# Four-column steps of the norms, the tangent and the ball on GpSimd in the first 14 of 16 groups, with a new order of the work

## The chip, the cores and the metric

The kernel runs on one core of a Trainium2 chip. The metric is the device time of one execution in microseconds; for the kernel before it is the median of three runs.

## The reference

128 graphs of 64 nodes, 256 features each, go through four layers. Each ends with the same residual and norm.

```python
x = _layernorm(x + gated_graph(x, adj, ...))    # 5 rounds: m = h @ W_l; agg = A^T m; h = GRU(agg, h)
x = _layernorm(x + graph_mlp(x, adj, ...))      # (eps * x + adj @ x) @ W1, RMS norm, silu, @ W2
x = _layernorm(x + project(expmap0(adj @ logmap0(x))))
x = _layernorm(x + attention(x, adj, ...))      # exp(e_i + f_j) on the edges, normalised, times h
```

The third layer is hyperbolic. `logmap0(x)` is the row `x` times `arctanh(min(n, 1 - 1e-7)) / n`, with `n` the row's length; the kernel calls it the tangent. `expmap0(u)` is `u` times `tanh(n)/n`, and `project` shortens rows that are longer than 0.996; together they are the ball. The layer norm subtracts the mean and divides by `sqrt(var + 1e-5)`. All of these need, for each row of 256 features, a few numbers only: mean, variance, length, factor.

## The kernel before, in words

**Tiles.** Two graphs make a block of 128 rows, which lie on the 128 partitions. Four blocks (`NB`) make a group, so there are 16 groups. A group's tile of rows is 128 x 4 x 256. A number for each row is a tile of 128 partitions x 4 columns (`tiny`), and a step on such a tile is called a four-column step here.

**What a group does**, in `group(g)`: five gated rounds (`gated`, matmuls at L800 and L806, in a Strassen-like form, with the sums of blocks `tA` and `tB` of `sums` made on VectorE, L345; between rounds VectorE transposes (L762) and 4 transfers (L675) bring the state back to rows as `hr`); the first norm; the aggregation and the two-layer network (`p_ah`, `p_bh`, `p_ch` at L983, squares at L969 whose sums GpSimd adds, L348, TensorE's `ps_ss` and a power on GpSimd at L1025, then scaling, silu and `ps_o`); the second norm; the tangent (L1051 to L1076), which scales the rows (L1080, L1081) for `ps_sup`; the ball (L1096 to L1112), which gives the factor `th` for the rows of L696; the third norm; the attention (`ps_a`, `ps_att`); the fourth norm and the output.

**The norm**, `layer_norm`: for groups 0 to 13 (`summed`) the row sums come with the sum that makes the rows. VectorE makes the mean with its sign turned (L712), ScalarE squares the rows around it and adds (L714), VectorE makes variance plus epsilon (L717), GpSimd raises it to −1/2 (L725, and to +1/2 for the second norm, which wants the row's length too), VectorE makes the length (L727) and the offset (L729). Groups 14 and 15 use VectorE's statistics instead of the sums (L721 to L723).

**The tangent and the ball.** VectorE limits the length, forms (1+n)/(1−n) with two reciprocals (L1053 to L1059); ScalarE takes Ln (L1061); VectorE sums a series for short rows (L1067 to L1072) and picks one of the two (L1074, L1076). In the ball GpSimd takes the root of the sum of squares (L1097), VectorE limits it (L1098), ScalarE takes tanh (L1099), and VectorE does a reciprocal (L1111) and six steps (L1105 to L1110).

**What sets the order.** Every operation is entered in a `Flow` with its engine, an estimated cost, and what it reads and writes. `Plan` then simulates the engines: it goes through time, and of the operations that are ready on each engine, from up to four groups at once (`WINDOW`), takes the one with the earliest start, and of several the first by a rank. `CHOICES` is a string of digits, one for each `STRETCH` microseconds of planned time, that says which rank counts there: group first, latest group first, or, for each entry of `LAGS`, the group's number times that lag less the longest path still ahead in the group. `HOPS` is what the plan adds between an operation and one on another engine that needs it. An operation marked `port` shares a port in the plan: GpSimd's and some of VectorE's don't overlap. The order found is then fixed for every engine's queue with dependencies (`BEHIND`); each engine works through its queue in that order, and an instruction that waits holds those behind it.

```python
    def pool(us, run, w, r=()):
        flow.op("POOL", us, run, w, r, port=True)
```

Of the kernel before, what the change touches and what calls it, by code (L numbers as in the profile page):

```python
# [128 lines left out]
class Flow:  # L129
# [11 lines left out]
    AHEAD = {"PE": 32, "DVE": 10, "ACT": 10, "POOL": 4, "SP": 2}  # L141


    HOPS = {"from PE": 0.22, "to PE": 0.15, "else": 0.06, "own": 0.0}

    SOONER = 0.4

# [2 lines left out]
    TRANSFERS = 8  # L150

    TABLE = 1.28
    WINDOW, STRETCH, LAGS = 4, 4.0, (60.0,)
    CHOICES = ("0001000220200211121122221102222222012010000101100010000000111101000111011110021011111000000111010210"
               "1211020210001002202110011000111212202011211020002100022200100101202020200112021110010111111000120211"
               "1102220002201010201110112001200101100101212111101011111001000010011100121121112020120101000000002220"
               "0010111020001121221202112100001010010120000001221112100000011000001001100000201221212001000010111110"
               "1101001100121020222110100210001101100000111100011011020110001000002010012201001001200010012002111101"
               "000201000111111111111102122110011000000100100110000111111011000011000")

    BEHIND = mybir.DependencyInfo(mybir.DependencyClass.NoSync, mybir.DependencyReason.DATA)

# [41 lines left out]
            u.then.append(o)  # L204
        self.ops.append(o)

    def hop(self, e, to):
        if e == to:
            return 0.0 if e == "PE" else self.HOPS["own"]
        return self.HOPS["from PE" if e == "PE" else "to PE" if to == "PE" else "else"]  # L210

    def ways(self):

        for i, o in enumerate(o for s in self.streams for o in s):
            o.id = i
        path = {}
        for ops in self.streams:
            longest = 0.0
            for o in reversed(ops):
                path[o] = o.us + max((path[u] + self.hop(o.eng, u.eng) for u in o.then if u.stream == o.stream), default=0.0)  # L220
                o.way = longest = max(longest, path[o])

    def issue(self):
# [17 lines left out]
def kernel(  # L241
# [31 lines left out]
    nc = tc.nc  # L273
    B, N, D = x.shape
# [3 lines left out]
    NB = 4  # L278
# [44 lines left out]
    def dve(n, run, w, r, port=False):  # L323
        flow.op("DVE", 0.145 + 0.00105 * n, run, w, r, port=port)
# [3 lines left out]
    def act(n, run, w, r, sets=None):  # L328
        flow.op("ACT", 0.22 + 0.00077 * n, run, w, r, sets=sets)
# [11 lines left out]
    def pool(us, run, w, r=()):  # L341
        flow.op("POOL", us, run, w, r, port=True)

    def summing(n, o, x0, x1, op, w, r):
        dve(n, lambda: nc.vector.tensor_tensor(o(), x0(), x1(), op), w, r, True)  # L345

# [21 lines left out]
    def over(t, n):  # L368
        return t.unsqueeze(1).to_broadcast([P, n, t.shape[-1]])
# [39 lines left out]
    eps2 = const.tile([P, 2, NB], F32, name="eps2")  # L409
# [214 lines left out]
    def group(g):  # L624
# [76 lines left out]
        def layer_norm(y, st, tag, name, norm=None):  # L701

            mv = tiny("mv", (P, NB, 2))
            ve, rstd, off = tiny("ve", (P, 2, NB)), tiny("rstd", (P, 2, NB)), tiny("off")
            o = rows(tag, f"x_{name}")
            m = 2 if norm else 1

            def row(b):
                return [(y, b)]

            if summed:
                dve(4, lambda: nc.vector.tensor_scalar(mv[:, :, 0], st[:, :, 0], -1.0 / D, None, OP.mult), [mv], [st])  # L712
                for b in range(NB):
                    act(400, lambda b=b: nc.scalar.activation(  # L714
                        o[:, b, :], y[:, b, :], AF.Square, bias=mv[:, b, 0:1], accum_out=st[:, b, 1:2]),
                        [(o, b), (st, (1, b))], [*row(b), mv])
                dve(8, lambda: nc.vector.scalar_tensor_tensor(  # L717
                    ve[:, :m, :], over(st[:, :, 1], m), 1.0 / D, eps2[:, :m, :NB], OP.mult, OP.add), [ve], [st])
            else:
                for b in range(NB):  # L720
                    dve(256, lambda b=b: nc.vector.bn_stats(st[:, b, :], y[:, b, :]), [(st, b)], row(b))  # L721
                    dve(4, lambda b=b: nc.vector.bn_aggr(mv[:, b, :], st[:, b, :]), [(mv, b)], [(st, b)])
                dve(8, lambda: nc.vector.tensor_tensor(  # L723
                    ve[:, :m, :], over(mv[:, :, 1], m), eps2[:, :m, :NB], OP.add), [ve], [mv])
            pool(1.25, lambda: nc.gpsimd.tensor_tensor(rstd[:, :m, :], ve[:, :m, :], pow2[:, :m, :NB], OP.pow), [rstd], [ve])  # L725
            if norm:
                dve(4, lambda: nc.vector.scalar_tensor_tensor(  # L727
                    norm.tile(), rstd[:, 1, :], float(np.sqrt(D)), rstd[:, 0, :], OP.mult, OP.mult), [norm], [rstd])
            dve(4, lambda: nc.vector.scalar_tensor_tensor(  # L729
                off.tile(), mv[:, :, 0], 1.0 if summed else -1.0, rstd[:, 0, :], OP.mult, OP.mult), [off], [mv, rstd])  # L730
# [306 lines left out]
        for h in range(2):  # L1037
# [11 lines left out]


        rn, fac, n2, ser = (tiny(t) for t in ("rn", "fac", "n2", "ser"))  # L1051
        near = tiny("near", dt=I32)
        dve(4, lambda: nc.vector.scalar_tensor_tensor(xn.tile(), xn.tile(), MIN_NORM, xn.tile(), OP.max, OP.max), [xn], [xn])  # L1053
        dve(4, lambda: nc.vector.reciprocal(rn.tile(), xn.tile()), [rn], [xn])
        dve(4, lambda: nc.vector.scalar_tensor_tensor(xn.tile(), xn.tile(), MAX_ARG, xn.tile(), OP.min, OP.min), [xn], [xn])

        dve(4, lambda: nc.vector.scalar_tensor_tensor(fac.tile(), xn.tile(), -1.0, one4[:, :NB], OP.mult, OP.add), [fac], [xn])
        dve(4, lambda: nc.vector.reciprocal(fac.tile(), fac.tile()), [fac], [fac])
        dve(4, lambda: nc.vector.scalar_tensor_tensor(fac.tile(), xn.tile(), 1.0, fac.tile(), OP.add, OP.mult),  # L1059
            [fac], [xn, fac])  # L1060
        act(4, lambda: nc.scalar.activation(fac.tile(), fac.tile(), AF.Ln), [fac], [fac], LN)  # L1061


        def series():
            v = nc.vector
            return [
                v.tensor_mul(n2.tile(), xn.tile(), xn.tile()),  # L1067
                v.scalar_tensor_tensor(ser.tile(), n2.tile(), 1.0 / 13.0, one4[:, :NB], OP.mult, OP.mult),
                *(v.scalar_tensor_tensor(ser.tile(), ser.tile(), 1.0 / q, n2.tile(), OP.add, OP.mult)
                  for q in (11, 9, 7, 5, 3)),  # L1070
                v.tensor_add(ser.tile(), ser.tile(), one4[:, :NB]),
                v.scalar_tensor_tensor(near.tile(), xn.tile(), SERIES_BELOW, one4[:, :NB], OP.is_lt, OP.mult)]  # L1072
        dve(1400, series, [n2, ser, near], [xn])
        dve(4, lambda: nc.vector.scalar_tensor_tensor(fac.tile(), fac.tile(), 0.5, rn.tile(), OP.mult, OP.mult),  # L1074
            [fac], [fac, rn])
        dve(4, lambda: nc.vector.copy_predicated(fac.tile(), near.tile(), ser.tile()), [fac], [fac, near, ser])  # L1076
        tan = rows("B", "tan")
        for b in range(NB):
            flow.either([
# [18 lines left out]
        dve(4, lambda: nc.vector.scalar_tensor_tensor(unb.tile(), un.tile(), MIN_NORM, un.tile(), OP.max, OP.max), [unb], [un])  # L1098
        act(64, lambda: nc.scalar.activation(th.tile(), unb.tile(), AF.Tanh), [th], [unb], TANH)  # L1099


        def onto_ball():
# [5 lines left out]
                v.reciprocal(un.tile(), un.tile()),  # L1108
                v.scalar_tensor_tensor(un.tile(), un.tile(), MAX_NORM, one4[:, :NB], OP.mult, OP.min),
                v.tensor_mul(th.tile(), th.tile(), un.tile())]  # L1110
        dve(4, lambda: nc.vector.reciprocal(urn.tile(), unb.tile()), [urn], [unb])  # L1111
        dve(900, onto_ball, [th, un], [th, un, urn])  # L1112
# [88 lines left out]
```

## Time and profile before

| What | Value |
|---|---|
| Median of 3 runs | 2306.16 us (2305.33 to 2307.16) |
| The profiled execution, its own time | 2305.08 us |
| Its span, first to last instruction | 2303.3 us |
| Granted clock of TensorE, mean | 0.993 |
| Busy: TensorE, VectorE, ScalarE, GpSimd | 2249.8, 1765.9, 1308.0, 339.1 us |

All views are of one profiled execution. PE is TensorE's matmul, PEld its weight load, DVE VectorE, ACT ScalarE, POOL GpSimd, SP SyncE. L696 is line 696 of the kernel; where a helper enters the operation, the line is the helper's, and the tile's name tells which step it is. In a row of groups the name after the operation is what is written, then what is read, then the shapes and the count; behind the bars stand the busy time, the mean of one in ns, and the idle time of the engine just before, with what ended it. In a timeline row the first two numbers are the start and the time in us. "x3" joins neighbouring instructions of one kind, and brackets hold the engine's idle time before and what ended it.

### The profile page before, as it was taken

To read this page: it belongs to the slowest core of one execution; us is meant where nothing else is said; L and a number is where in the kernel's file an instruction comes from. 1 tells how busy PE (TensorE), PEld (TensorE's weight loads), DVE (VectorE), ACT (ScalarE), POOL (GpSimd) and SP (SyncE) were. 2 spreads that over 40 slices of the span, in tenths; PEclk is the share of its full clock that TensorE was granted. 3 is DMA by queue.
4 is the path that set the end of the run, shared out by engine and by line. 5 is a ranking of instruction groups with operands and counts; after the bars stand their busy time and mean duration, and the time that the engine had idled before them with its cause. 6 is when DMAs were issued, how large, how long until landed. Compare 5 with 4: busy or idle time off the path is not lost.

```text
span 2303.3 us, 32320 instructions
## 1 busy us (share of the span) xinstructions
PE 2249.8 (98%) x11242; PEld 1973.5 (86%) x11242; DVE 1765.9 (77%) x4167; ACT 1308.0 (57%) x2797; POOL 339.1 (15%) x272
## 2 busy tenths in 40 slices
PE   9999999999999999999999999999999999999995
PEld 7888888888888888888788888888888888888874
DVE  6777788778688777777677778777877787867876
ACT  3444556665655555556565556646555566555564
POOL 2100202310110200202021021201110230110011
PEclk9999999999999999999999999999999999999997
DMA  5221112122213022102212212212122112212200
GB/s 145 28 33 28 28 23 54 19 49 28 49 28 58 10 31 55 28 19 40 46 40 28 49 28 30 47 19 48 29 28 45 32 19 49 54 14 28 46 10 19
DMA packets 428770, 84.20 MB, mean 37 GB/s; under 512 B 399124, under 2 KB 427824, under 8 KB 428608
## 3 DMA queue, kind: packets, MB, share of 16 engines
q1 hardware_dynamic: 426880, 80.26, 19.8%
q8 instruction: 89, 1.46, 0.3%
q10 hardware_dynamic: 1328, 1.31, 0.2%
q0 software_dynamic: 400, 0.57, 0.1%
q14 instruction: 73, 0.60, 0.1%
HBM read 32.55 MB, written 8.39 MB: 18 GB/s over the span
## 4 chain that ended last, share of the span: by engine, by line
PE 89%; DVE 6%; DMA 2%; SPq 1%; issue 1%; ACT 1%; POOL 0%; POOLq 0%; ACTq 0%; DVEq 0%
PE p_ga L800 22%; PE p_gc L800 11%; PE ps_o L315 9%; PE ps_agg L315 7%; PE p_hx L806 6%; PE p_gb L800 5%; PE p_ix L806 5%; PE p_ah L983 4%; PE p_iy L806 4%; PE p_hy L806 4%; PE ps_a L315 2%; PE p_ch L983 2%; DMA hr<-t 1%; SPq L675 1%; PE ps_wmih L315 1%; PE ps_sup L315 1%
## 5 line engine op out<-in xcount | busy, mean ns | idle before, releaser
L725 POOL TENSOR_TENSOR rstd<-ve,pow 128x4 f32<-128x4 f32 (+1 forms) x64 | 78.3, 1224 | 1097.5 <-DVE ve L717 1012.3
L315 PE MATMUL ps_o<-w2s,hid 128*128 128x256 f32 x1024 | 232.3, 379 | 0.4 <-ACT hid L1034 0.3
L315 PEld LDWEIGHTS ps_o<-w2s,hid 128*128 128x128 f32 x1024 | 193.8, 190 | 27.7 <-ACT hid L1034 1.5
L338 ACT ACTIVATE hnb<-p_hx,half_b 128x256 f32<-128x256 f32 x215 | 101.4, 471 | 146.1 <-PE p_hx L806 102.5
L800 PE MATMUL p_gc<-tA,w_h 128*128 128x256 f32 x640 | 172.4, 381 | 2.4 <-DVE y L696 2.4
L800 PE MATMUL p_ga<-tA,w_h 128*128 128x256 f32 x640 | 173.1, 379 | 0.0
L800 PE MATMUL p_gc<-tB,w_a 128*128 128x256 f32 x640 | 172.6, 380 | 0.2 <-DVE tB L345 0.2
L800 PE MATMUL p_ga<-tB,w_a 128*128 128x256 f32 x640 | 168.0, 379 | 0.7 <-DVE tB L345 0.7
L800 PE MATMUL p_ga<-agg,w_a 128*128 128x256 f32 x640 | 166.5, 379 | 0.0
L800 PE MATMUL p_ga<-hT,w_h 128*128 128x256 f32 x640 | 166.4, 379 | 0.0
L315 PEld LDWEIGHTS ps_agg<-edge,hr 128*128 128x128 f32 x1024 | 142.6, 192 | 24.5 <-issue 7.1
L315 PE MATMUL ps_agg<-edge,hr 128*128 128x128 f32 x1024 | 148.1, 278 | 7.0 <-DMA hr<-t 4.6
L853 ACT ACTIVATE U<-U,half_b 128x512 f32<-128x512 f32 (+1 forms) x160 | 94.3, 628 | 76.4 <-DVE U L850 76.3
L800 PEld LDWEIGHTS p_gc<-tA,w_h 128*128 128x128 f32 x640 | 120.9, 191 | 18.7 <-DVE y L696 2.8
L800 PEld LDWEIGHTS p_ga<-tB,w_a 128*128 128x128 f32 x640 | 120.6, 190 | 17.4 <-DVE tB L345 1.3
L800 PEld LDWEIGHTS p_gc<-tB,w_a 128*128 128x128 f32 x640 | 120.3, 190 | 16.5 <-DVE tB L345 0.8
L800 PEld LDWEIGHTS p_ga<-agg,w_a 128*128 128x128 f32 x640 | 119.9, 190 | 16.9 <-issue 1.0
L800 PEld LDWEIGHTS p_ga<-hT,w_h 128*128 128x128 f32 x640 | 119.2, 190 | 15.7 <-issue 0.5
L333 ACT COPY agg<-ps_agg 128x512 f32<-128x512 f32 x141 | 81.6, 579 | 87.8 <-PE ps_agg L315 85.4
L800 PEld LDWEIGHTS p_ga<-tA,w_h 128*128 128x128 f32 x640 | 117.2, 190 | 13.6
L853 ACT ACTIVATE V<-V,half_b 128x256 f32<-128x256 f32 (+1 forms) x160 | 86.6, 585 | 58.5 <-DVE V L850 58.1
L866 DVE TENSOR_TENSOR V<-p_ix,V 128x256 f32<-128x256 f32 x192 | 80.5, 419 | 33.5 <-PE p_ix L806 30.3
(261 smaller groups left out, 5466.0 us busy)
## 6 DMA issues: line engine op xcount, KB each, us to landing
hr<-t SPq DMA_DIRECT2D x256, 128.0 KB, 3.7
x<-in_x_dram SPq DMA_DIRECT2D x64, 128.0 KB, 2.6
xr<-in_x_dram SPq DMA_DIRECT2D x16, 512.0 KB, 4.3
out_dram<-x_n SPq DMA_DIRECT2D x16, 512.0 KB, 3.0
xs<-in_x_dram SPq DMA_DIRECT2D x120, 64.0 KB, 2.5
x3T<-t SPq DMA_DIRECT2D x56, 128.0 KB, 3.8
edge<-in_adj_dram SPq DMA_DIRECT2D x64, 32.0 KB, 2.2
wm<-in_L_gnn_weight_dram SPq DMA_DIRECT2D x5, 256.0 KB, 3.4
```

The lines of the kernel that those rows point to most:

```text
L315: return nc.tensor.matmul(o, lhsT, rhs, start=(k == 0), stop=(k == nk - 1))
L333: flow.either([("ACT", 0.22 + 0.00077 * n, lambda: nc.scalar.copy(o(), i())), ("DVE", 0.145 + 0.00105 * n, lambda: nc.vector.tensor_copy(o ...
L338: flow.either([("ACT", 0.3 + 0.0008 * n, lambda: nc.scalar.activation(o(), i(), AF.Identity, bias=bias(), scale=scale())), ("DVE", 0.145 + ...
L675: flow.op("SP", 0.6, lambda q=q: nc.sync.dma_start(view(dst.tile())[:, q], t[W * q:W * (q + 1)].rearrange("r m x d -> r m (x d)")), [(dst, ...
L725: pool(1.25, lambda: nc.gpsimd.tensor_tensor(rstd[:, :m, :], ve[:, :m, :], pow2[:, :m, :NB], OP.pow), [rstd], [ve])
L800: pe(HR, lambda i=i, w=w, c=c: nc.tensor.matmul(ps[:, c * HR:(c + 1) * HR], w[:, m, c * P:(c + 1) * P], v[i][0](), start=first and i == 1 ...
L806: pe(HR, lambda: nc.tensor.matmul(ps[:, j * HR:(j + 1) * HR], w[:, m, :], v[0](), start=first, stop=True, skip_group_check=True), [ps], [( ...
L853: act(HR if len(w) == 1 else R, lambda: nc.scalar.activation(o(), src(), AF.Tanh, bias=half_b[:, i * KD + c:i * KD + c + 1], scale=0.5), w ...
L866: dve(HR + 44, lambda: nc.vector.tensor_add(uu[:, c, half(n)], region(ps, j), uu[:, c, half(n)]), [(uu, (n, c))], [ps, (uu, (n, c))])
L983: pe(HR, lambda c=c: nc.tensor.matmul(ps[:, c * HR:(c + 1) * HR], w1f[:, w, (2 * q + c) * P:(2 * q + c + 1) * P], v[0](), start=first and ...
```

## The change

In the groups 0 to 13 nearly all four-column steps of the norms, the tangent and the ball go from VectorE to GpSimd. Two helpers, `few` and `few_s`, enter them with a planned cost of 0.25 us. Reciprocals become powers of −1, of which two share one instruction in the tangent. VectorE's fused steps fall apart into plain ones: a step of the series is a product and a sum, and the choice between Ln and series becomes `fac + near * (ser - fac)`. Groups 14 and 15 keep the old code. The planner's addition for a result on its way to TensorE goes from 0.15 to 0.42 us (the old value, as `REACH`, still serves for the longest paths), `STRETCH` goes from 4 to 7 us, `LAGS` has a second entry, and `CHOICES` is a new string of 328 digits in place of 569, so the order of all engines' queues is new.

```diff
-    HOPS = {"from PE": 0.22, "to PE": 0.15, "else": 0.06, "own": 0.0}
+    HOPS = {"from PE": 0.22, "to PE": 0.42, "else": 0.06, "own": 0.0}
+
+    REACH = {"from PE": 0.22, "to PE": 0.15, "else": 0.06, "own": 0.0}
...
-    WINDOW, STRETCH, LAGS = 4, 4.0, (60.0,)
...
+    WINDOW, STRETCH, LAGS = 4, 7.0, (60.0, 150.0)
...
-                path[o] = o.us + max((path[u] + self.hop(o.eng, u.eng) for u in o.then if u.stream == o.stream), default=0.0)
+                path[o] = o.us + max((path[u] + self.hop(o.eng, u.eng, self.REACH) for u in o.then if u.stream == o.stream), default=0.0)
...
+    def few(w, x0, x1, op, r):
+
+        pool(0.25, lambda: nc.gpsimd.tensor_tensor(w[0](), x0(), x1(), op), [w[1]], r)
+
+    def few_s(w, x, s0, op0, r, s1=None, op1=None):
+
+        pool(0.25, lambda: nc.gpsimd.tensor_scalar(w[0](), x(), s0, s1, op0, *((op1,) if op1 else ())), [w[1]], r)
...
+    less2 = const.tile([P, 2, NB], F32, name="less2")
+    nc.vector.memset(less2, -1.0)
...
-                dve(4, lambda: nc.vector.tensor_scalar(mv[:, :, 0], st[:, :, 0], -1.0 / D, None, OP.mult), [mv], [st])
+                few_s((lambda: mv[:, :, 0], mv), lambda: st[:, :, 0], -1.0 / D, OP.mult, [st])
...
-                dve(8, lambda: nc.vector.scalar_tensor_tensor(
-                    ve[:, :m, :], over(st[:, :, 1], m), 1.0 / D, eps2[:, :m, :NB], OP.mult, OP.add), [ve], [st])
+                few_s((lambda: ve[:, 0, :], (ve, 0)), lambda: st[:, :, 1], 1.0 / D, OP.mult, [st], LN_EPS, OP.add)
+                if norm:
+                    few_s((lambda: ve[:, 1, :], (ve, 1)), lambda: st[:, :, 1], 1.0, OP.mult, [st])
...
+            if summed:
+                few((lambda: off.tile(), off), lambda: mv[:, :, 0], lambda: rstd[:, 0, :], OP.mult, [mv, rstd])
+                if norm:
+                    few((lambda: norm.tile(), norm), lambda: rstd[:, 1, :], lambda: rstd[:, 0, :], OP.mult, [rstd])
+            else:
+                if norm:
+                    dve(4, lambda: nc.vector.scalar_tensor_tensor(
+                        norm.tile(), rstd[:, 1, :], float(np.sqrt(D)), rstd[:, 0, :], OP.mult, OP.mult), [norm], [rstd])
                 dve(4, lambda: nc.vector.scalar_tensor_tensor(
-                    norm.tile(), rstd[:, 1, :], float(np.sqrt(D)), rstd[:, 0, :], OP.mult, OP.mult), [norm], [rstd])
-            dve(4, lambda: nc.vector.scalar_tensor_tensor(
-                off.tile(), mv[:, :, 0], 1.0 if summed else -1.0, rstd[:, 0, :], OP.mult, OP.mult), [off], [mv, rstd])
+                    off.tile(), mv[:, :, 0], -1.0, rstd[:, 0, :], OP.mult, OP.mult), [off], [mv, rstd])
...
+        if summed:
+            near, lim, inv = tiny("near"), tiny("lim"), tiny("inv", (P, 2, NB))
+            few_s((lambda: lim.tile(), lim), lambda: xn.tile(), MIN_NORM, OP.max, [xn], MAX_ARG, OP.min)
+            few_s((lambda: inv[:, 0, :], (inv, 0)), lambda: lim.tile(), -1.0, OP.mult, [lim], 1.0, OP.add)
+            few_s((lambda: inv[:, 1, :], (inv, 1)), lambda: xn.tile(), MIN_NORM, OP.max, [xn], 2.0, OP.mult)
+            few_s((lambda: n2.tile(), n2), lambda: lim.tile(), 1.0, OP.add, [lim])
+            pool(1.25, lambda: nc.gpsimd.tensor_tensor(inv.tile(), inv.tile(), less2[:, :, :NB], OP.pow), [inv], [inv])
+            few((lambda: fac.tile(), fac), lambda: n2.tile(), lambda: inv[:, 0, :], OP.mult, [n2, inv])
+            act(4, lambda: nc.scalar.activation(fac.tile(), fac.tile(), AF.Ln), [fac], [fac], LN)
+            few((lambda: n2.tile(), n2), lambda: lim.tile(), lambda: lim.tile(), OP.mult, [lim])
+            few_s((lambda: ser.tile(), ser), lambda: n2.tile(), 1.0 / 13.0, OP.mult, [n2], 1.0 / 11.0, OP.add)
+            for q in (9, 7, 5, 3, 1):
+                few((lambda: ser.tile(), ser), lambda: ser.tile(), lambda: n2.tile(), OP.mult, [ser, n2])
+                few_s((lambda: ser.tile(), ser), lambda: ser.tile(), 1.0 / q, OP.add, [ser])
+            few_s((lambda: near.tile(), near), lambda: lim.tile(), SERIES_BELOW, OP.is_lt, [lim])
+            few((lambda: fac.tile(), fac), lambda: fac.tile(), lambda: inv[:, 1, :], OP.mult, [fac, inv])
+            few((lambda: ser.tile(), ser), lambda: ser.tile(), lambda: fac.tile(), OP.subtract, [ser, fac])
+            few((lambda: ser.tile(), ser), lambda: ser.tile(), lambda: near.tile(), OP.mult, [ser, near])
+            few((lambda: fac.tile(), fac), lambda: fac.tile(), lambda: ser.tile(), OP.add, [fac, ser])
...
+        if summed:
+            few_s((lambda: unb.tile(), unb), lambda: un.tile(), MIN_NORM, OP.max, [un])
...
+        if summed:
+            pool(1.04, lambda: nc.gpsimd.tensor_tensor(urn.tile(), unb.tile(), less2[:, 0, :NB], OP.pow), [urn], [unb])
+            few((lambda: th.tile(), th), lambda: th.tile(), lambda: urn.tile(), OP.mult, [th, urn])
+            few((lambda: un.tile(), un), lambda: th.tile(), lambda: un.tile(), OP.mult, [th, un])
+            few_s((lambda: un.tile(), un), lambda: un.tile(), MIN_NORM, OP.max, [un])
+            pool(1.04, lambda: nc.gpsimd.tensor_tensor(un.tile(), un.tile(), less2[:, 0, :NB], OP.pow), [un], [un])
+            few_s((lambda: un.tile(), un), lambda: un.tile(), MAX_NORM, OP.mult, [un], 1.0, OP.min)
+            few((lambda: th.tile(), th), lambda: th.tile(), lambda: un.tile(), OP.mult, [th, un])
+        else:
+            dve(4, lambda: nc.vector.reciprocal(urn.tile(), unb.tile()), [urn], [unb])
+            dve(900, onto_ball, [th, un], [th, un, urn])
```

More of the change, by code (lines that the diff above doesn't have):

```diff
@@ L152 @@
     TABLE = 1.28
-    WINDOW, STRETCH, LAGS = 4, 4.0, (60.0,)
[L154 to L159, printed above, removed]
+    WINDOW, STRETCH, LAGS = 4, 7.0, (60.0, 150.0)
+    CHOICES = ("0010032202000010000101000000100101200211212021110210210022212000010021010211122100122212200010120021"
+               "0210111100010100200111200121100102102211102100100010001002101010121001100100121112200201010102002100"
+               "1010101001102000211100212100110100021110222020000101220210121200200010100201210100110111010011010111"
+               "1000111101110110111001011000")
     BEHIND = mybir.DependencyInfo(mybir.DependencyClass.NoSync, mybir.DependencyReason.DATA)
@@ L205, in either, with hop @@
         self.ops.append(o)
-    def hop(self, e, to):
+    def hop(self, e, to, hops=None):
+        hops = hops or self.HOPS
         if e == to:
-            return 0.0 if e == "PE" else self.HOPS["own"]
-        return self.HOPS["from PE" if e == "PE" else "to PE" if to == "PE" else "else"]
+            return 0.0 if e == "PE" else hops["own"]
+        return hops["from PE" if e == "PE" else "to PE" if to == "PE" else "else"]
     def ways(self):
@@ L725, in layer_norm @@
             pool(1.25, lambda: nc.gpsimd.tensor_tensor(rstd[:, :m, :], ve[:, :m, :], pow2[:, :m, :NB], OP.pow), [rstd], [ve])
-            if norm:
+            if summed:
[6 more added lines that the diff above has]
+                        norm.tile(), rstd[:, 1, :], float(np.sqrt(D)), rstd[:, 0, :], OP.mult, OP.mult), [norm], [rstd])
                 dve(4, lambda: nc.vector.scalar_tensor_tensor(
-                    norm.tile(), rstd[:, 1, :], float(np.sqrt(D)), rstd[:, 0, :], OP.mult, OP.mult), [norm], [rstd])
-            dve(4, lambda: nc.vector.scalar_tensor_tensor(
-                off.tile(), mv[:, :, 0], 1.0 if summed else -1.0, rstd[:, 0, :], OP.mult, OP.mult), [off], [mv, rstd])
+                    off.tile(), mv[:, :, 0], -1.0, rstd[:, 0, :], OP.mult, OP.mult), [off], [mv, rstd])
             for b in range(NB):
@@ L1051, in group @@
         rn, fac, n2, ser = (tiny(t) for t in ("rn", "fac", "n2", "ser"))
[L1052 to L1076, printed above, removed]
+        if summed:
[18 more added lines that the diff above has]
+        else:
+            near = tiny("near", dt=I32)
+            dve(4, lambda: nc.vector.scalar_tensor_tensor(xn.tile(), xn.tile(), MIN_NORM, xn.tile(), OP.max, OP.max), [xn], [xn])
+            dve(4, lambda: nc.vector.reciprocal(rn.tile(), xn.tile()), [rn], [xn])
+            dve(4, lambda: nc.vector.scalar_tensor_tensor(xn.tile(), xn.tile(), MAX_ARG, xn.tile(), OP.min, OP.min), [xn], [xn])
+            dve(4, lambda: nc.vector.scalar_tensor_tensor(fac.tile(), xn.tile(), -1.0, one4[:, :NB], OP.mult, OP.add), [fac], [xn])
+            dve(4, lambda: nc.vector.reciprocal(fac.tile(), fac.tile()), [fac], [fac])
+            dve(4, lambda: nc.vector.scalar_tensor_tensor(fac.tile(), xn.tile(), 1.0, fac.tile(), OP.add, OP.mult),
+                [fac], [xn, fac])
+            act(4, lambda: nc.scalar.activation(fac.tile(), fac.tile(), AF.Ln), [fac], [fac], LN)
+            def series():
+                v = nc.vector
+                return [
+                    v.tensor_mul(n2.tile(), xn.tile(), xn.tile()),
+                    v.scalar_tensor_tensor(ser.tile(), n2.tile(), 1.0 / 13.0, one4[:, :NB], OP.mult, OP.mult),
+                    *(v.scalar_tensor_tensor(ser.tile(), ser.tile(), 1.0 / q, n2.tile(), OP.add, OP.mult)
+                      for q in (11, 9, 7, 5, 3)),
+                    v.tensor_add(ser.tile(), ser.tile(), one4[:, :NB]),
+                    v.scalar_tensor_tensor(near.tile(), xn.tile(), SERIES_BELOW, one4[:, :NB], OP.is_lt, OP.mult)]
+            dve(1400, series, [n2, ser, near], [xn])
+            dve(4, lambda: nc.vector.scalar_tensor_tensor(fac.tile(), fac.tile(), 0.5, rn.tile(), OP.mult, OP.mult),
+                [fac], [fac, rn])
+            dve(4, lambda: nc.vector.copy_predicated(fac.tile(), near.tile(), ser.tile()), [fac], [fac, near, ser])
@@ L1097, in group @@
         pool(1.04, lambda: nc.gpsimd.tensor_tensor(un.tile(), us.tile(), p_half[:, :NB], OP.pow), [un], [us])
-        dve(4, lambda: nc.vector.scalar_tensor_tensor(unb.tile(), un.tile(), MIN_NORM, un.tile(), OP.max, OP.max), [unb], [un])
+        if summed:
+            few_s((lambda: unb.tile(), unb), lambda: un.tile(), MIN_NORM, OP.max, [un])
+        else:
+            dve(4, lambda: nc.vector.scalar_tensor_tensor(unb.tile(), un.tile(), MIN_NORM, un.tile(), OP.max, OP.max), [unb], [un])
         act(64, lambda: nc.scalar.activation(th.tile(), unb.tile(), AF.Tanh), [th], [unb], TANH)
@@ L1110, in onto_ball @@
                 v.tensor_mul(th.tile(), th.tile(), un.tile())]
-        dve(4, lambda: nc.vector.reciprocal(urn.tile(), unb.tile()), [urn], [unb])
-        dve(900, onto_ball, [th, un], [th, un, urn])
+        if summed:
[6 more added lines that the diff above has]
+            few((lambda: th.tile(), th), lambda: th.tile(), lambda: un.tile(), OP.mult, [th, un])
+        else:
+            dve(4, lambda: nc.vector.reciprocal(urn.tile(), unb.tile()), [urn], [unb])
+            dve(900, onto_ball, [th, un], [th, un, urn])
         st2 = stats()
```

## The prediction, made before the changed kernel had run

> **What bounds the kernel now.** I read the page's first part, then the table of stages, then the starts of the matmuls in the timeline, and last the timeline around the longest gaps.
>
> ```profile
> PE 2249.8 (98%) x11242; PEld 1973.5 (86%) x11242; DVE 1765.9 (77%) x4167; ACT 1308.0 (57%) x2797; POOL 339.1 (15%) x272
> ```
>
> TensorE has work for 98% of the span, and the change touches none of it. So only its idle time can be won. The stages say where that lies (busy us of PE, PEld, DVE, ACT, POOL in each stretch):
>
> ```profile
> core 0: us, PE busy (x) PEld busy (x) DVE busy (x) ACT busy (x) POOL busy (x), PEclk, DMA share, GB/s
> 0.00:144.00 144.00, 141.52 (x687) 118.95 (x688) 99.38 (x215) 58.32 (x125) 26.55 (x48) 1.00 0.32 75
> 144.00:1008.00 864.00, 857.61 (x4315) 757.03 (x4313) 670.43 (x1528) 487.87 (x1035) 117.74 (x85) 1.00 0.21 35
> 1008.00:1152.00 144.00, 137.09 (x669) 119.13 (x670) 107.61 (x281) 95.88 (x217) 26.86 (x19) 0.98 0.20 35
> 1152.00:2160.00 1008.00, 1001.27 (x5035) 883.49 (x5034) 783.05 (x1840) 584.55 (x1256) 147.59 (x105) 1.00 0.20 35
> 2160.00:2256.00 96.00, 92.23 (x459) 79.14 (x459) 76.69 (x187) 58.45 (x106) 11.87 (x8) 1.00 0.10 23
> 2256.00:2303.30 47.30, 20.05 (x83) 15.74 (x82) 28.73 (x120) 22.91 (x60) 8.49 (x7) 0.73 0.07 23
> ```
>
> Idle: 27.3 us in the last 47 us, where only the last two groups are left, and 26.2 us before. Busy time hides more: a 256-column matmul is recorded as 379 ns, but the next starts 216 ns after it (8 in 1.73 us in the chain), so a delay of up to 160 ns doesn't show. From the starts themselves, time beyond the usual spacing is 64.9 us, 26.3 of it in the last sixteenth of the span, so **38.6 us before that**. The last two groups keep the old operations (`summed` is false for them). The 38.6 us is what the change can work on; 14.9 us of all the gaps is in 171 pieces under 0.2 us, the rest in some 55 larger ones.
>
> What stands in front of the larger ones:
>
> ```profile
> 1128.05 0.66 DVE L345 TENSOR_TENSOR tA<-hT 128x512 f32<-128x512 f32 x1
> 1128.62 0.15 DVE L1105 TENSOR_TENSOR th<-th,rn 128x4 f32<-128x4 f32 x1
> ...
> 1129.61 0.16 DVE L1110 TENSOR_TENSOR th<-th,n 128x4 f32<-128x4 f32 x1
> ...
> 1130.76 2.07 PE L800 MATMUL p_gc<-tA,w_h 128*128 128x256 f32 x4 [2.39 <-DVE y L696]
> ...
> 1131.63 0.42 DVE L345 TENSOR_TENSOR tA<-hT,tA 128x256 f32<-128x256 f32 x1
> ```
>
> Six four-column operations of the ball (1.2 us) and the four rows behind them sit between two sums that TensorE needs; it waits 2.39 us. Another:
>
> ```profile
> 1022.63 2.37 POOL L348 TENSOR_TENSOR xb<-x_n,b_r 128x1024 f32<-128x1024 f32 x1 [2.29 <-ACT x_n L338]
> 1022.70 2.33 DVE L1059 SCALAR_TENSOR_TENSOR fac<-n,fac 128x4 f32<-128x4 f32 x1
> ...
> 1028.26 0.70 PE L806 MATMUL p_iy<-tB,w_in 128*128 128x256 f32 x2 [1.00 <-DVE V L866]
> ```
>
> A 0.16 us operation of the tangent takes 2.33 us because it meets a wide GpSimd sum; VectorE's queue stands behind it, and TensorE pays 1.00 us. The same pattern is at 446 to 451 us (three locked four-column operations, then PE gaps of 0.4 and 1.7 us) and at 1859 us (three, then 1.1 us). By the starts the four places come to about 7 us of the 38.6.
>
> **The change, part by part.**
>
> *Taken from VectorE.* Per group 3 for each of four norms and 1 more for the second (13), 17 of the tangent, 8 of the ball: 38, in 14 groups 532. Their rows, with 14/16 of those that the last two groups share:
>
> ```profile
> L1069 DVE SCALAR_TENSOR_TENSOR ser<-ser,n 128x4 f32<-128x4 f32 x80 | 15.0, 188 | 2.7
> L729 DVE SCALAR_TENSOR_TENSOR off<-mv,rstd 128x4 f32<-128x4 f32 x64 | 11.0, 172 | 10.0 <-POOL rstd L725 10.0
> ```
>
> Tangent rows L1053 to L1076 sum to 50.4 us, so 44; ball rows L1098 and L1105 to L1111 20.9, so 18; norms (L712, L717, L727, L729) 9.2+9.8+3.2+9.6 = 32. In all 94 us, 5% of VectorE's 1766. 9 of the 10 small operations that met a wide GpSimd sum are among them (mean 188 where most take 162). Idle time at the head of the queue goes too: L729, L727 and L1098 wait 24 us, nearly all for powers on GpSimd. None of this counts directly, since VectorE is not the bound; it counts in the 7 us above.
>
> *Put on GpSimd.* Per group 14 steps for the norms, 22 for the tangent, 6 for the ball: 42, in all 588; and three powers more (8 columns at 1.64, two of 4 at 1.01: 3.65 us, in all 51). No four-column step other than a power is in the trace. The nearest rows are chains of three dependent sums:
>
> ```profile
> 43.32 1.52 POOL L434 TENSOR_TENSOR w_in<-w_in 128x128 f32<-128x128 f32 x3 [0.56 <-ACT w_in L338]
> 48.02 2.35 POOL L434 TENSOR_TENSOR w_a<-w_a 128x256 f32<-128x256 f32 x3 [1.85 <-DVE w_a L339]
> ```
>
> 0.507 and 0.783 us a step, pause included: 0.276 for 128 columns, so 0.23 is fixed, and four columns take 0.24 (estimate). The Trainium skill speaks against the move: its page GPSIMD Engine Reference, section Performance versus the Vector engine, has GpSimd about twice as slow elementwise, with two software hops ahead of each instruction. Twice the 0.16 of the rows, and the pause of 0.08, would be 0.40. So 141 us by the rows, 235 by the rule; I take the rows, since at four columns the fixed part is all. GpSimd goes from 339 to about 530 us (23%); by the rule 27%. Neither binds. Bounds on TensorE's time: 0, and the queue case below.
>
> *The port.* The Trainium skill, page SBUF — State Buffer, section SBUF: two separate sides, says that VectorE's operations with two SBUF inputs and GpSimd's share a pair of ports, and whichever starts keeps the pair for its whole instruction. The wide sum above bears this out. For a power it doesn't:
>
> ```profile
> 962.21 1.13 POOL L1025 TENSOR_TENSOR fac<-rn,m_half 128x4 f32<-128x4 f32 x1 [2.42 <-DVE rn L1023]
> 962.72 0.68 DVE L345 TENSOR_TENSOR tA<-hT 128x512 f32<-128x512 f32 x1
> ```
>
> The sum with two SBUF inputs keeps its 0.68 us inside the power. By the rule the 51 us of new powers, met by VectorE's such operations (about 30% of the span, L345, L857, L923, L925), would cost it 15 us; by the rows 0, which I take. A short step can hold VectorE for 0.24 us at most and be held up to 0.69 by it.
>
> *Latency.* The tangent took 3.2 us from power to factor where nothing disturbed it (2260.5 to 2263.7). Now 6 steps, a power and its pause of 0.08, 13 steps beside the Ln, 4 more: 23 x 0.24 + 1.7 = 7.2. The ball goes from 1.6 to 6 x 0.24 + 2 x 1.08 = 3.6. With the norms' hops some 6.5 us a group. At nothing, since up to four groups are in flight and TensorE works on the others; without that cover it costs up to 6.5 us each time. Only the last two groups lack it, and they keep the old chain.
>
> *New waits.* GpSimd's factor step waits for ScalarE's Ln (with its table load of 1.28 us). Queued behind it are the sums of squares, which TensorE's `ps_ss` needs, and powers of other groups. ScalarE's Square now waits for GpSimd's mean, with ScalarE at 57%. SP's queue and the DMAs are the same in kind, and their place follows the order.
>
> *The order anew.* The planner now charges 0.42 instead of 0.15 for a result on its way to TensorE, so it leaves room before a matmul. This can take small gaps; I give it half of the 14.9 us, 7. It also reshuffles the tail (26 us by gaps, 11 after the last matmul): from −6 to +6, taken as 0. The extra memset (62 ns) is nothing.
>
> **Sum.** −7 (small operations ahead of needed sums) − 7 (small gaps) + 3.5 (new meetings at the port and waits in GpSimd's queue: a quarter of what is won, my choice; bounds 0 and the 18 us of the last rival) = −10.5. Span 2303.3 → 2292.8; with the 1.8 us outside it (2305.08 − 2303.3) 2294.6; the median 2306.16 is 1.1 above the profiled run, so **2296 us**.
>
> **Rivals.** (The measurement tells about 0.2%, 4.6 us, from no change.)
> - *The forecast*, 2288 to 2301: 0.48.
> - *A better order*: with VectorE freer, `hr` transposes and their transfers leave earlier, and TensorE's waits on `hr` (8 us by gaps) and a quarter of the 20 us then left (5) go too: −23.5, 2283. For it, these are late because VectorE is late; against it, TensorE's gaps have many owners: 0.22.
> - *It does nothing measurable*: gaps move elsewhere, since VectorE was idle 23% anyway and the tail, 27 us, is as before: 2305, 0.20.
> - *Slower*: GpSimd's queue. If the step behind Ln stands 1.28 us (the table load) and the sums of squares behind it arrive that late at TensorE in each of 14 groups, 18 us is lost, against 10.5 won: 2314. It decides from (10.5 + 4.6)/14 = 1.1 us a group. For it, GpSimd's waits for ScalarE are long (up to 46 us at L1097) and its queue is in order; against it, planned order and 77% idle time: 0.10.
>
> Range 2281 to 2309: it leaves out the best of the second case (0.08) and most of the last (0.09). Faster 0.70, same 0.20, slower 0.10.
>
> **What would show it.** VectorE near 1672 us, no locked four-column operation before the last two groups; GpSimd near 530 with short steps at 0.15 to 0.3 us; gaps before the last sixteenth at 28 us instead of 38.6; the tail within 6 us. Wrong if short steps take over 0.4 us, if `ps_ss` or `ps_sup` waits on GpSimd appear in TensorE's list, or if the tail moves by more than the middle.

## The result, and the profile after

The changed kernel takes **2296.92 us** (median of 5 runs, 2296.39 to 2298.3) against 2306.16 us (5 runs, 2304.79 to 2307.64): ratio 0.9961, 95% interval 0.9947 to 0.9976. The forecast was 2296. The profiled execution took 2296.92 us with a span of 2295.1, 8.2 less than before. The total came out right, by luck: the gaps ahead of the last sixteenth fell by 7 us more than forecast, and those in it grew by 10 us where nothing was forecast.

The first part of the page after:

```profile
PE 2245.7 (98%) x11242; PEld 1979.1 (86%) x11242; DVE 1696.8 (74%) x3633; ACT 1308.8 (57%) x2800; POOL 554.3 (24%) x902
```

TensorE has the same 11242 matmuls. VectorE lost 69 us and 534 instructions, GpSimd gained 215 us and 630. Where TensorE's time went shows in three stretches, first of after, then of before (us of the stretch, then busy us of PE, PEld, DVE, ACT, POOL, then the granted clock):

```profile
144.00:2008.00 1864.00, 1857.31 (x9374) 1648.52 (x9373) 1389.35 (x2918) 1098.28 (x2364) 476.31 (x785) 1.00 0.18 36
2008.00:2295.10 287.10, 251.03 (x1204) 216.01 (x1202) 208.22 (x499) 153.82 (x315) 50.27 (x69) 0.95 0.11 23
```
```profile
144.00:2008.00 1864.00, 1843.98 (x9255) 1624.86 (x9254) 1444.18 (x3395) 1087.79 (x2343) 276.25 (x197) 1.00 0.21 36
2008.00:2303.30 295.30, 264.28 (x1303) 229.68 (x1302) 222.32 (x560) 161.88 (x329) 36.31 (x27) 0.96 0.14 24
```

In the same 1864 us of the middle 119 more matmuls run, and TensorE is idle for 6.7 us instead of 20.0. In the last stretch the idle time is 36 us instead of 31, for fewer matmuls. Counted from the starts of the matmuls, as in the prediction, and split at 0.5 us a gap:

| beyond the usual spacing, us (gaps) | before | after | order alone (below) |
|---|---|---|---|
| up to 144 us | 2.9 (30) | 7.1 (28) | 8.4 (32) |
| 144 to 2016 us, gaps under 0.5 us | 15.6 (127) | 4.6 (43) | 8.9 (71) |
| 144 to 2016 us, larger gaps | 19.8 (17) | 7.1 (7) | 8.9 (8) |
| from 2016 us on, gaps under 0.5 us | 6.2 (45) | 11.8 (87) | 12.2 (81) |
| from 2016 us on, larger gaps | 20.4 (7) | 26.4 (11) | 26.1 (11) |
| sum | 64.9 | 57.0 | 64.6 |

So 23.7 us were won in the middle and 15.8 given back at the two ends; 7.9 is left, against 8.2 of the span. (Two runs below keep after's order and steps in the middle, the one with the dots later and the one with both; they have 4.5 and 6.3 us in the second row, so a difference under 2 us in one row says little.) The four-column steps on GpSimd, the groups of after (busy us, mean ns | idle before them):

```profile
L351 POOL TENSOR_SCALAR ser<-ser 128x4 f32<-128x4 f32 x70 | 20.4, 292 | 6.1
L347 POOL TENSOR_TENSOR ser<-ser,n 128x4 f32<-128x4 f32 x70 | 19.7, 282 | 5.8
L347 POOL TENSOR_TENSOR off<-mv,rstd 128x4 f32<-128x4 f32 x56 | 13.3, 237 | 4.3
L347 POOL TENSOR_TENSOR fac<-fac,inv 128x4 f32<-128x4 f32 x14 | 5.2, 368 | 22.4 <-ACT fac L1077 22.2
L1075 POOL TENSOR_TENSOR inv<-inv,less 128x8 f32<-128x8 f32 x14 | 23.6, 1686 | 0.0
```

588 steps take 159 us: median 220 ns, mean 271, at most 762. The fourth row is the feared step behind Ln. It waits there six times, for 22.2 us in all (us, times):

```profile
  ACT fac L1077: 22.2, 6
```

But no row of GpSimd's factors or sums of squares is in TensorE's list of waits (us in total, times, longest), which names only the last step ahead of TensorE:

```profile
PE ps_T L668 <- ACT x_n L339: 5.9, 1, 5.9
PE ps_sup L316 <- DVE tan L1118: 5.3, 1, 5.3
PE ps_o L316 <- ACT hid L1051: 4.3, 3, 2.2
PE p_hy L823 <- DVE y L707: 3.7, 1, 3.7
...
PE ps_agg L316 <- DVE a_t L621: 2.6, 1, 2.6
```

The first two are in the last two groups, the fourth is at 2156 us, the last ends at 76 us: four of the five rows shown belong to the ends. Of the seven larger gaps that are left in the middle, three (at 237, 780 and 1586 us, 3.1 of the 7.1 us) stand behind an operation of VectorE that is held by one of GpSimd's wide sums, which were there before the change.

### The profile page after: what moved, and what is told of

The parts are those of the page before. It is cut to its first block, busy times and chain, and to the rows that moved or that the text cites. A ratio compares the mean times of both kernels' runs of the same rounds, so it can differ in the third digit from the quotient of the medians.

```text
span 2295.1 us, 32440 instructions
## 1 busy us (share of the span) xinstructions
PE 2245.7 (98%) x11242; PEld 1979.1 (86%) x11242; DVE 1696.8 (74%) x3633; ACT 1308.8 (57%) x2800; POOL 554.3 (24%) x902
## 4 chain that ended last, share of the span: by engine, by line
PE 93%; DVE 3%; ACT 1%; POOL 1%; DMA 1%; issue 1%; SPq 0%; POOLq 0%; ACTq 0%; DVEq 0%
PE p_ga L817 23%; PE p_gc L817 12%; PE ps_o L316 9%; PE ps_agg L316 7%; PE p_ix L823 6%; PE p_gb L817 6%; PE p_hx L823 6%; PE p_ah L1000 4%; PE p_hy L823 4%; PE p_iy L823 4%; PE ps_a L316 2%; PE p_ch L1000 2%; PE ps_att L316 1%; PE ps_sup L316 1%; PE p_bh L1000 1%; PE ps_wmih L316 1%
## 5 line engine op out<-in xcount | busy, mean ns | idle before, releaser
L351 POOL TENSOR_SCALAR mv<-st 128x4 f32<-128x4 f32 x56 | 15.6, 278 | 829.5 <-DVE y L707 442.0
L316 PE MATMUL ps_agg<-edge,hr 128*128 128x128 f32 x1024 | 143.5, 276 | 2.8 <-DVE a_t L621 2.6
L817 PEld LDWEIGHTS p_gc<-tB,w_a 128*128 128x128 f32 x640 | 121.0, 190 | 17.8 <-DVE tB L354 1.6
```

The source lines that it names most:

```text
L316: return nc.tensor.matmul(o, lhsT, rhs, start=(k == 0), stop=(k == nk - 1))
L351: pool(0.25, lambda: nc.gpsimd.tensor_scalar(w[0](), x(), s0, s1, op0, *((op1,) if op1 else ())), [w[1]], r)
L817: pe(HR, lambda i=i, w=w, c=c: nc.tensor.matmul(ps[:, c * HR:(c + 1) * HR], w[:, m, c * P:(c + 1) * P], v[i][0](), start=first and i == 1 ...
```

## Experiments

The change has two parts, steps on another engine and a new order. My theory was the prediction's: part of the gain is relief of VectorE, part is the order's, and the longer chain of the steps costs nothing. The rivals: all of it is the order; or the chain costs, and the order buys it back.

**The order alone.** The order of after stays fixed; the 588 steps, not the powers, are issued by VectorE at the places that the plan gave them on GpSimd.

```diff
-        pool(0.25, lambda: nc.gpsimd.tensor_tensor(w[0](), x0(), x1(), op), [w[1]], r)
+        pool(0.25, lambda: nc.vector.tensor_tensor(w[0](), x0(), x1(), op), [w[1]], r)
+        flow.ops[-1].real = "DVE"
...
+            eng = o.real or eng
```

> The changed kernel with its own order, but the 588 short steps (not the powers) issued by VectorE at the places that they have in the plan. If what counts is that VectorE's queue is free of them, VectorE rises from 1697 to about 1790 us busy, locked four-column steps and waits for powers and Ln at the head of its queue come back, and the time goes to 2306 or above (2306 to 2325). If the new order alone made the gain, it stays within 3 us of 2297.

Measured: 2302.75 us, ratio 0.9988 (0.9979 to 0.9997), between the two outcomes that I had named; VectorE is busy for 1760.8 us. The order alone brings about 3 us, the steps on GpSimd about 6 (5.8 between the medians, 7.5 between the profiled spans). Two limits: VectorE does the new, unfused steps here (588, where before had 532) with the added powers still on GpSimd, and the order was planned for steps on GpSimd. The table has the place: against this kernel, after has 4.3 us less in small gaps of the middle and only 1.8 less in large ones there.

**The moved steps alone.** The kernel before, its order kept; the steps of the norms, the tangent and the ball take their GpSimd form at their old places.

```diff
+    def moved_dve(n, old, new, w, r):
+        dve(n, new if summed_now[0] else old, w, r)
+        if summed_now[0]:
+            flow.ops[-1].real = "POOL"
```

> The kernel before with its own order on every engine, but the four-column steps of groups 0 to 13 issued by GpSimd in their new form at the places that they had. If a freed VectorE is worth something by itself, about 7 us of gaps go and 0 to 4 come back from GpSimd's queue: 2299 to 2303. If only the order that was found for it pays, 2306 or above, since GpSimd's queue was not planned for the steps.

Measured: 2317.79 us, ratio 1.0055 (1.004 to 1.007). 12 us slower, where I had expected a gain: the steps without an order made for them lose. Gaps in the middle went from 35.4 us to 48.0, nearly all of it in large ones (19.8 to 31.0). Two ways lead there. They are in the timeline, first at the largest of the new gaps, then at the prediction's first place, where TensorE waited 2.39 us before and 3.47 us now:

```profile
455.18 0.22 POOL L356 TENSOR_SCALAR ser<-ser 128x4 f32<-128x4 f32 x1
455.37 0.23 POOL L356 TENSOR_SCALAR near<-lim 128x4 f32<-128x4 f32 x1
455.56 1.26 POOL L362 TENSOR_TENSOR sqt<-sqt,sqh 128x512 f32<-128x512 f32 x1
456.86 0.72 ACT L988 ACTIVATE sqh<-hid,cols 128x512 f32<-128x512 f32 x1 [3.99 <-POOL sqt L362]
457.48 0.46 ACT L339 ACTIVATE hnb<-p_hy,half_b 128x256 f32<-128x256 f32 x1
...
457.99 1.22 PE L825 MATMUL p_hy<-tA,w_hn 128*128 128x256 f32 x2 [3.40 <-ACT hnb L339]
...
1138.23 0.20 POOL L353 TENSOR_TENSOR th<-th,n 128x4 f32<-128x4 f32 x1
1138.46 0.48 DVE L713 SCALAR_TENSOR_TENSOR y<-ps_sup,th,x_n 128x256 f32<-128x256 f32 x1 [2.44 <-POOL th L353]
...
1139.41 0.92 PE L819 MATMUL p_gc<-tA,w_h 128*128 128x256 f32 x3 [3.47 <-DVE y L713]
```

At 455 a sum of squares stands behind the series in GpSimd's queue; ScalarE's next square waits 3.99 us for it, and the `hnb` pass behind that, which has nothing to do with either, is what TensorE needs. That is the in-order queue of the prediction's last rival, though behind the series and not behind Ln. At 1138 VectorE stands 2.44 us for the ball's factor, with the work behind it that TensorE waits for: the longer chain itself, which the prediction took at nothing. Of the next four new gaps (at 1103, 1242, 1405 and 1948 us, 2.0 to 2.8 us each) the first is of the first kind, the other three are of the second. Under an order not made for the steps the two decide the sign.

**The chain twice as long.** After, each short step issued twice, first onto a spare tile; the plan still charges 0.25 us.

```diff
-        pool(0.25, lambda: nc.gpsimd.tensor_tensor(w[0](), x0(), x1(), op), [w[1]], r)
+        pool(0.25, lambda: [nc.gpsimd.tensor_tensor(spare, x0(), x1(), op),
+                            nc.gpsimd.tensor_tensor(w[0](), x0(), x1(), op)], [w[1]], r)
```

> The changed kernel, each of its 588 short steps on GpSimd done a second time onto a spare tile just before it. GpSimd gains some 120 to 140 us, a group's chains some 5 us. If their length and port use are hidden, as the prediction took them, the time stays within 3 us of 2297. If GpSimd's queue or the port reaches TensorE, 10 us or more are added (2307 and above).

Measured: 2402.24 us, ratio 1.0417 (1.040 to 1.0435): 105 us more than after, 7.5 a group. The 588 added steps take 143 us of GpSimd, which stays idle for 71% of the span; the time that VectorE's operations lost while they met GpSimd's (what they took above the median of their form) rose from 28.4 to 32.0 us only. What is late, in the list of TensorE's waits (us in total, times, longest) and in the idle time before `ps_sup`, where matmuls and weight loads both count (us, times):

```profile
PE ps_sup L316 <- ACT tan L1120: 35.0, 10, 6.5
```
```profile
  ACT tan L1120: 73.9, 20
```

So the longer chain is not hidden by the other groups: the kernel fixes every queue's order, and TensorE can't take other work in place of the `ps_sup` that is next. What covers a chain is the distance that the plan put between its ends. `ps_sup` is a third of the 105 us; the rest is spread over many waits that I did not follow. GpSimd's queue grows with the chain in this run, so it doesn't part the one from the other.

**The same search for all four.** Old or new steps, 0.15 or 0.42 us to TensorE; all else of the planner as in after, and one search through its choices for each of the four. (The order in after comes from another, so these four compare with each other.)

```diff
-    HOPS = {"from PE": 0.22, "to PE": 0.15, "else": 0.06, "own": 0.0}
-    WINDOW, STRETCH, LAGS = 4, 4.0, (60.0,)
+    HOPS = {"from PE": 0.22, "to PE": 0.42, "else": 0.06, "own": 0.0}
+    WINDOW, STRETCH, LAGS = 4, 7.0, (60.0, 150.0)
```

> The old operations, in an order found by one and the same search (a beam of 180, digits of 7 us, two lags) with 0.15 us for a result on its way to TensorE. The plan ends its last matmul at 2280.6 us. In the kernel before the chip came 22.9 us after its plan (2292.0 against 2269.1), in the changed one 4.4 (2284.1 against 2279.7). If the 0.15 makes the plan blind to gaps, the last matmul ends near 2303 and the run takes about 2316 us. If the price of the hop doesn't matter, all four of these runs come equally far after their plans, by some 12 us: 2306.

> The same search, the old operations, 0.42 us. The plan ends at 2308.4 us. If 0.42 makes the plan truthful, the chip comes about 5 us after it, last matmul near 2313, run about 2326 us. If the price doesn't matter: 12 us after it, 2333.

> The same search, the new operations on GpSimd, 0.15 us. The plan ends at 2277.0 us, 3.6 before that of the old operations. If 0.15 makes the plan blind: last matmul near 2300, run about 2313 us. If the price doesn't matter: 2302.

> The same search, the new operations, 0.42 us. The plan ends at 2304.7 us. If 0.42 makes the plan truthful: last matmul near 2309, run about 2322 us. If the price doesn't matter: 2329.

| median us (ratio to before, interval) | 0.15 us | 0.42 us |
|---|---|---|
| old steps | 2328.65 (1.0099, 1.0084 to 1.0114) | 2329.62 (1.0101, 1.0086 to 1.0116) |
| new steps | 2310.65 (1.0019, 1.0012 to 1.0025) | 2321.12 (1.0065, 1.0048 to 1.0082) |

The new steps win in both columns, by 18.0 and 8.5 us, but only the 18.0 is won in the middle. From 144 to 2016 us the gaps fall from 39.2 to 26.0 us at 0.15, and rise from 26.7 to 30.4 at 0.42, where the gain is from 2016 us on (55.9 to 47.7). The 0.42 wins in neither row, and it doesn't take the small gaps of the middle either: 13.4 us at 0.15 and 11.5 at 0.42 with the old steps, 11.1 and 11.9 with the new. What it does is make the plan true: the last matmul ends on the chip later than the plan has it by 35.4 and 22.9 us at 0.15 (old, new), by 5.1 and 4.1 at 0.42; in the two real kernels by 22.9 (before, 2269.1 planned, 2292.0 on the chip) and 4.4 (after, 2279.7 and 2284.1). Three of the four forecasts for a price that matters were within 4 us; old steps at 0.15 came 13 us later. A truthful price didn't pay for itself here: the room that it leaves is planned instead of suffered. Each cell is one order, so the luck of a search is in these differences.

**Which steps matter.** After with its order; the norms' 14 steps a group, or the tangent's 22, issued by VectorE again.

```diff
+            back[0] = True
...
+        v = back[0]
+        pool(0.25, lambda: (nc.vector if v else nc.gpsimd).tensor_tensor(w[0](), x0(), x1(), op), [w[1]], r)
+        flow.ops[-1].real = "DVE" if v else None
```

> The changed kernel with its own order, the 14 steps a group of the norms back on VectorE at their places in the plan, those of the tangent and the ball on GpSimd. If bursts of the tangent and the ball ahead of needed sums are what the move takes away, the time stays within 2 us of 2297. If the norms' waits for powers at the head of VectorE's queue count, it comes near the 2303 of the run with all steps on VectorE.

> The changed kernel with its own order, the 22 steps a group of the tangent back on VectorE at their places in the plan, those of the norms and the ball on GpSimd. All steps back cost 5.9 us, the norms' alone 0.7. If the tangent's bursts are the rest, as three of the prediction's four places have it, this comes to 2301 or 2302. If the ball's steps ahead of needed sums are, it stays near 2297.

Norms: 2297.58 us, ratio 0.9961 (0.9947 to 0.9974), no difference from after. Tangent: 2301.99 us, 0.9981 (0.9972 to 0.999), 5.1 us above after. The tangent is most of the 5.8 (by the ratios, each against its own runs of before, 4.6 of 6.2 us; its interval just touches that of after, and its profiled span is 4.7 longer). The ball's steps were not run alone. The timeline of the tangent's run shows how it happens, first with the steps on VectorE, then after, at the same place in the work:

```profile
835.88 0.16 DVE L351 TENSOR_TENSOR fac<-n,inv 128x4 f32<-128x4 f32 x1 [0.18 <-POOL inv L1083]
836.07 0.16 DVE L351 TENSOR_TENSOR n<-lim 128x4 f32<-128x4 f32 x1
...
836.76 0.59 ACT L335 COPY agg<-ps_agg 128x512 f32<-128x512 f32 x1
837.22 0.70 PE L830 MATMUL p_hx<-tA,w_hn 128*128 128x256 f32 x2 [0.50 <-DVE hnb L341]
...
838.40 0.17 DVE L357 TENSOR_SCALAR ser<-ser 128x4 f32<-128x4 f32 x1
838.48 0.68 DVE L361 TENSOR_TENSOR tB<-agg 128x512 f32<-128x512 f32 x1
```
```profile
834.79 0.60 PE L823 MATMUL p_hx<-tA,w_hn 128*128 128x256 f32 x2
834.99 0.58 ACT L334 COPY agg<-ps_agg 128x512 f32<-128x512 f32 x1
835.61 0.69 DVE L354 TENSOR_TENSOR tB<-agg 128x512 f32<-128x512 f32 x1 [0.76 <-ACT agg L334]
835.74 0.62 POOL L347 TENSOR_TENSOR ser<-ser,n 128x4 f32<-128x4 f32 x1
```

In the first, `agg` is there at 837.35 and the sum that reads it starts 1.13 us later, behind the series; `p_hx` waits 0.50 us for the `hnb` step that the first four pushed back. In the second, the sum starts 0.04 us after `agg`, `p_hx` doesn't wait, and the series runs on GpSimd, one of its steps held to 0.62 us while the sum has the port.

**The ends.** A new order from 1995 us of the plan on, in finer digits; the attention dots (`a_t`) of the head spread later in VectorE's queue; and both.

```diff
-        for c in self.CHOICES:
+        for c in self.CHOICES[:self.LAST]:
...
+        for c in self.TAIL:
+            until += self.FINE
```
```diff
+        for e, o in plan.order:
+            if o.late:
+                held.append((e, o))
+                continue
+            order.append((e, o))
+            if held and e == "DVE":
+                n += 1
+                if n > 8 and n % 3 == 0:
+                    order.append(held.pop(0))
```

> The changed kernel up to 1995 us of planned time; from there an order looked for with digits of 1.75 us and two more lags. The plan ends 2.4 us earlier (2277.3 against 2279.7). If the plan with 0.42 is truthful in the tail too: 2294.5. If the chip's tail is set by what the plan doesn't know (TensorE's lower speed after a stop), no change or some us either way.

> The changed kernel with one shift: the set-up products of the attention (rows of a_t, at 74.8 us behind a transfer) are spread over VectorE's queue from 8 instructions later on, one after every third. If they cost the 2.75 us that TensorE waits there: 2294. If the queue's work is only put off: 2297.

> Both of the above: 2292 if both hold and add up, 2297 if neither does.

Tail: 2295.3 us, 0.995 (0.9937 to 0.9964), 1.6 below after with intervals that overlap; the gaps from 2016 us on fell from 38.2 to 35.1 us, nearly all in large ones. Dots: 2296.57, 0.9958 (0.9946 to 0.9971), no gain. Both: **2293.38**, 0.9946 (0.9933 to 0.9958): the lowest median of all, 3.5 below after, though the intervals of the two overlap. The dots were a misreading of mine. In after, TensorE's wait at 76 us has a dot as its releaser; with the dots out of the way the same wait names a transfer (first after, then the dots later):

```profile
76.11 0.47 ACT L339 ACTIVATE hnb<-p_hx,half_b 128x256 f32<-128x256 f32 x1 [5.07 <-DMA hr<-t]
76.17 1.13 PE L316 MATMUL ps_agg<-edge,hr 128*128 128x128 f32 x8 [2.58 <-DVE a_t L621]
```
```profile
75.68 1.13 PE L326 MATMUL ps_agg<-edge,hr 128*128 128x128 f32 x8 [2.35 <-DMA hr<-t]
```

The first row shows what it was: ScalarE's pass waits for the same transfer and starts 0.06 us before the matmul, as it does with the dots later (75.62 and 75.68). The transfer was what TensorE waited for, and no part of the wait is shown to be the dot's.

## Why the prediction was right, and where it was not

The total was right, by mechanisms partly as told and two errors that cancelled. Ahead of the last sixteenth the gaps fell by 17.8 us (38.6 to 20.8) where I had 10.5, and those in it grew by 9.9 where I had 0. That the two came out together near −8 is luck.

- **Small operations ahead of needed sums, −7:** the mechanism was right, the size in part luck. With the new order fixed, moving the steps is worth 5.8 us. But I had counted four places with large gaps; the gain sits mainly in the small gaps of the middle (4.3 us, against 1.8 in large ones), and of the 12.7 us that went from the larger gaps the order took 10.9 with the steps still on VectorE. It is mostly in one family of steps: the tangent's unbroken run, 5.1 us, the norms next to nothing. In the old order the same move costs 12 us.
- **Small gaps, −7, put down to the price of 0.42:** the small gaps of the middle fell by 11.0 us, 6.7 of it with the order alone, so the size was right for the middle. The cause isn't the price, as far as the runs show: with an equal search 0.42 gains nothing, in these gaps or in all.
- **The tail, ±6, taken as 0:** the step that failed, and with it one of the signs that I had named ("the tail within 6 us"). The gaps of the last sixteenth of the span (after, from 2151.7 us on) rose from 26.3 to 36.2 us. The head, which I had not priced, lost 4.2, and 1.7 more went between 2016 us and the last sixteenth. All this was hidden because the order also won 10.9 us in large gaps of the middle, a gain that I had given only to a rival (the better order). So the order won 17.6 us in the middle and lost 17.2 at both ends by the gaps of the profiled runs; between the medians it is ahead by about 3.
- **Port and queue, +3.5:** not found. By the same measure VectorE's operations lost 32.6 us before and 28.4 after; GpSimd's queue makes no wait in TensorE's list. The rival of the stalled factor step had its stall (22.2 us in six places, where it had put 1.28 in each of 14) and, in the new order, no victim that the list shows; in the old order the queue is behind the largest new gap. Where the port still shows in the larger gaps of the middle, it is held by GpSimd's wide sums, not by the steps.
- **Latency at nothing:** right as a number for this kernel, wrong as a reason. "Other groups cover it" is refuted by the doubled steps (+7.5 us a group) and by the moved steps in the old order (+12 us). Where the order was planned with it, no wait for the tangent or the ball of groups 0 to 13 is in TensorE's list.
- **Gaps before the last sixteenth, 28 us:** 20.8, a gain of 17.8 and not 10.5; the large gaps that the order won are the difference.
- **VectorE −94 us, to 1672:** its operations on one to eight columns fell from 150.9 to 55.6 us, 95.3. Busy time only fell by 69, to 1697. 8 us are other work: 7.6 more in copies (11 more of them), 5.1 more of wide operations held at the port, and less of some others. The rest, 18 us, is in the records: those of short steps overlap their neighbours' (the `th` at 1128.62 in the prediction's fence begins before the sum ahead of it ends, 1128.71), so the sum of the rows was more than they added to the busy time.
- **GpSimd about 530 us, a step at 0.24:** 554. A clear step takes 0.19 to 0.23 us with a pause of 0.08 behind it, some 0.29 from one to the next; my 0.24 had the pause in it, so it was low, and the 141 us made from it counted the pauses as busy time (159 without them). The mean of 0.27 is from 115 steps held over 260 ns, nearly all while VectorE has the port; with the pause it is 0.35. The Trainium skill's factor of two (GPSIMD Engine Reference, Performance versus the Vector engine) had come to an estimate of 0.40 with the pause: the rows were nearer for a clear step, the page for the mean.
- **A power holds no port:** right again after, for VectorE. The sums of L354 (128x512, two SBUF inputs) that lie inside a power keep their 0.68 us (9 of them, mean 682 ns), against the rule of the page SBUF — State Buffer. But a power waits for the port at its start, which I had not seen. Of the 27 powers after that start while VectorE is in the midst of such an operation, 24 take over 0.12 us more than the shortest of their size; of the other 111 none does:

```profile
1210.34 0.69 DVE L874 SCALAR_TENSOR_TENSOR V<-V,hnb 128x512 f32<-128x512 f32 x1
1210.50 1.41 POOL L1042 TENSOR_TENSOR fac<-rn,m_half 128x4 f32<-128x4 f32 x1 [3.15 <-DVE rn L1040]
```

- **No locked four-column operation before the last two groups:** right. Of 11 small operations that lost 11.3 us before, two are left (2.0 us), both `ser<-ser,hw` of two columns, which was not moved.

Open: whether after's worse ends come from the luck of its search or from pricing 0.42. The tail's new order recovered 1.6 to 3.5 us of about 12 by the medians, with intervals that overlap after's, and the head's `hr` transfer was not tried on its own.

## What to carry to other kernels

Moving tiny operations to an idle engine paid here where they form an unbroken run ahead of work that the bound engine needs; look for the run, not for the sum of busy time. With queues in a fixed order a longer chain is hidden only as far as the order was planned for it, so move the steps and plan anew together, and test each alone. The name in a list of waits can be the wrong one; look for another engine whose wait ends at the same moment. A gain in the middle is checked against the two ends of the span before its size is believed.

## What the runs showed of the hardware

A four-column step took 0.16 us on VectorE and 0.19 to 0.23 on GpSimd when undisturbed; a power took 1.0 us for four columns and 1.64 for eight, so 0.16 for each further column.

TensorE's clock halved after some stops, and later than the stop. After, in fine stretches around the wait at 2156 us, then behind one at 2198 us, then the first 144 us; last before, behind the wait at 1128 us (columns as above, and behind the clock the DMA share and GB/s):

```profile
2155.00:2160.00 5.00, 1.28 (x7) 0.80 (x5) 4.93 (x10) 0.00 (x0) 0.00 (x0) 1.00 0.32 52
2160.00:2161.50 1.50, 0.37 (x2) 0.00 (x0) 1.33 (x8) 0.00 (x0) 0.00 (x0) 0.72 0.99 160
2161.50:2163.00 1.50, 1.45 (x6) 1.39 (x7) 1.40 (x9) 0.47 (x1) 0.00 (x0) 0.50 0.16 28
2163.00:2166.00 3.00, 3.00 (x13) 2.73 (x12) 2.90 (x12) 1.09 (x4) 0.23 (x1) 0.50 0.01 3
2166.00:2170.00 4.00, 4.00 (x21) 3.59 (x20) 1.28 (x4) 2.54 (x6) 1.03 (x1) 0.81 0.00 0
...
2202.00:2205.50 3.50, 3.50 (x18) 3.47 (x18) 1.90 (x3) 2.71 (x6) 2.06 (x1) 0.57 0.00 0
...
0.00:144.00 144.00, 137.32 (x667) 114.56 (x668) 99.23 (x217) 56.69 (x122) 27.76 (x48) 1.00 0.31 75
```
```profile
1130.70:1137.50 6.80, 4.98 (x15) 3.93 (x16) 3.92 (x14) 3.13 (x10) 1.01 (x1) 0.50 0.41 59
```

TensorE stood for 3.7 us with the clock at 1.00, until 2159.7. The means of 0.72 and 0.81 put the halving near 2160.7, 1 us after the work was back, and the full clock near 2167.5: 6.8 us at half, with another stop of 1.2 us among them. The Trainium skill (TensorE: Matmul & The Clock Gate, Part 1: The HAM clock gate) has half clock after an idle window of about 3.4 us, and full after as long a busy one. The stop fits; the time at half was twice as long. Shorter waits can do it too: 2.7 us at 2198 us was followed by a stretch at 0.57, and 2.39 us at 1128 us before by 6.8 us at 0.50, while 2.6 us up to 76 us after was followed by none. What tells these apart no run here shows. In the last sixteenth about 31 matmuls of 256 columns' worth ran 0.21 us longer each, against 8 before: some 5 us of its 9.9.
